# A three-pass graph kernel: destinations compared once per block, and groups taken in pairs in the third pass

## The chip, the cores and the metric

The kernel runs on one core of one Trainium2 chip. The metric is device time in microseconds from start to end on that core. The engines are named as the profile names them: PE is TensorE (matmul; its weight loads are PEld), DVE is VectorE, ACT is ScalarE, POOL is GpSimd, and SP is SyncE, which here only issues DMAs. Each engine works through its own queue in order. They wait for one another through semaphores, counters that an instruction raises when it is done.

## The reference

Two graph layers run over 30000 nodes of 128 features and 960000 edges, all in float32. The edges are sorted by destination.

```
h  = relu(layernorm(x))
# layer 0: a relation convolution with 32 edge types, used twice
W   = einsum('rb,bdf->rdf', coeff, basis)            # 32 matrices out of 8
agg = segment_sum((h @ W[etype])[src] * weight, dst) + bias
h1  = relu(agg(h; basis1, coeff1));   x = x + agg(h1; basis2, coeff2)
# layer 1: a gate with 4 edge types t
h   = relu(layernorm(x))
eta = sigmoid((h @ Wk[t] + bk[t])[dst] + (h @ Wq[t] + bq[t])[src])
out = x + mean over t of (segment_sum(eta * (h @ Wv[t] + bv[t])[src], dst) + h @ Ws[t] + b[t])
```

## The kernel before

Each of the two relation convolutions and the gate is one pass over all edges. A tile is 128 edges, a group is 3 tiles (G = 3, 384 edges), and a block is 5 groups (S = 5). One iteration of a pass's hardware loop holds 20 blocks (100 groups), cut into 4 stages of 25 groups; there are 25 iterations. Because edges are sorted, the destinations of a group lie in a window of 32 neighbouring nodes (W = 32) that starts at a number read from memory, its base.

**A relation pass** (`rel_body`, lines 415 to 541). For each group POOL gathers the source rows of 3 tiles with an indirect DMA each (line 511, recorded at line 118 in the helper), into `hg`, which has five buffers. DVE makes for each tile a matrix `sb` of 128 edges by 8 x 32 columns (line 515): where an edge's destination `relc` equals the column number `iw`, it holds the edge's coefficient `ce`, else 0. PE multiplies `hg` with `sb` and sums the 3 tiles in PSUM, in `pa` (line 520). ACT copies `pa` into `ab` (line 524). After the second group of a block PE runs `bases_out` for the block before (line 479): 8 matmuls with the basis matrices into `po`. At the fourth group DVE adds `po` of two blocks ago onto the node array `agg`, five windows (`add_windows`, line 413). The `sb` pool has 12 buffers, four groups.

In the first pass the edge types of a block are also loaded (`types`, line 436, four DMAs with 512-byte rows), compared with the type numbers (`onehot`, line 444) and multiplied with the coefficients (line 449) at the fourth group. That matmul writes the columns `pc` of a PSUM tile `cp`; the column numbers `iw` lie in the same tile, as do the partition numbers `ic`. The coefficients of the second pass are stored along the way and loaded back there (`keep`, `kept`).

**The gate pass** (`gate_body`, lines 543 to 631). For each group SP loads 128 rows of keys (`window`, line 560), five groups ahead. PE picks the key of each edge with a one-hot matrix (`keys`, line 577) into `pk`, which has four buffers. POOL gathers query and value (`qv`, ten buffers, line 614, again recorded at line 118). DVE adds the query (line 618), ACT takes the sigmoid (line 619). Two groups later DVE multiplies with the value (`msg`, line 586) and PE sums by destination into `po` (line 588). The order in DVE's queue is thus: add of group n, msg of group n-2; once a block also a one-hot comparison of 1920 columns with the destination matrix `sel` of 480 columns (lines 564, 570), and the five window adds.

All three passes run node steps beside the edges (`beside`): every 9 groups a unit of 120 nodes is turned, normalised, multiplied or stored, a few instructions per group. The order of the instructions on each engine is the order in which the program writes them; the framework adds only the semaphores. [...] The relation passes use `po` 2, `pa` 3, node steps 2 and `cp` 1; the gate pass uses `pk` 4, `po` 2, node steps 1 and `cp` 1.

Of the kernel before, what the change touches and what calls it, by code (L numbers as in the profile page):

```python
# [9 lines left out]
F32 = mybir.dt.float32  # L10
# [3 lines left out]
ALU = mybir.AluOpType  # L14
# [35 lines left out]
NX = N + LAG  # L50
LEAD = 3 * VB
GAP = 8
EPS = 1e-5
CH = 5
PX, KX = 120, 10
# [17 lines left out]
def kernel(  # L73
# [261 lines left out]
    def sorted_path():  # L335
# [5 lines left out]
        with ExitStack() as all_:  # L341
            def edge_pass(name, body, after, banks, extra=None):


                with ExitStack() as held:
                    weights = held.enter_context(tc.tile_pool(name=f"{name}_w", bufs=1))
                    steps, run = after(weights), body(weights)
                    with tc.tile_pool(name=f"{name}_io", bufs=NQ) as io, \
                            tc.tile_pool(name=f"{name}", bufs=2) as pool, \
                            tc.tile_pool(name=f"{name}_n", bufs=1) as npool, \  # L350
                            tc.tile_pool(name=f"{name}_nps", bufs=banks, space=PSUM) as nps, \
                            tc.tile_pool(name=f"{name}_c", bufs=1, space=PSUM) as cps, \
                            tc.tile_pool(name=f"{name}_ps", bufs=2, space=PSUM) as ps:
                        cp = cps.tile([P, 4 * D], F32, name="cp")
                        iw, ic = cp[:, :W], cp[:, W:W + 1]
                        nc.vector.tensor_copy(iw, irow)
                        nc.vector.tensor_copy(ic, icol)
                        with tc.For_i(0, NI, 1, iteration_sync="staggered") as i:
                            with tc.manual_schedule():
                                todo = {}  # L360
                                for n, step_ in extra(i, npool) if extra else ():
                                    todo.setdefault(n, []).append(step_)
                                for u in range(NPI // VB):
                                    at = i * -NPI + (N + LAG - (u + 1) * VB)
                                    for n, step in steps(at, npool, nps, 2):
                                        todo.setdefault(u * PERIOD + n, []).append(step)
                                assert W < TQ * 8 * B and max(todo) < NG

                                def beside(n):
                                    for step in todo.get(n, ()):  # L370
                                        step()

                                run(i, io, pool, ps, cp, iw, ic, beside)
                    left = LAG // VB
                    with tc.tile_pool(name=f"{name}_l", bufs=left) as lpool, \
                            tc.tile_pool(name=f"{name}_lps", bufs=8, space=PSUM) as lps:
                        for together in zip(*(steps(at, lpool, lps, left)
                                              for at in range(0, LAG, VB))):
                            for _, step in together:
                                step()  # L380
# [34 lines left out]
            def rel_body(table, weights, second):  # L415
                def start(npool):
                    bas = npool.tile([P, B, D], F32, name="bas")
                    nc.scalar.dma_start(bas, weights.rearrange("b d f -> d b f"))
                    return lambda *args: body(bas, *args)

                def body(bas, i, io, pool, ps, cp, iw, ic, beside):
                    stage = {}
                    er, oh, pc, ce, ce_next, ab, po, base = {}, {}, {}, {}, {}, {}, {}, {}

# [7 lines left out]

                    def types(s):
                        er[s] = pool.tile([P, TQ, TP], I32, name="er")
                        for c in range(TQ):
                            nc.sync.dma_start(
                                er[s][:, c, :],
                                bass.AP(tensor=et32_row.tensor,
                                        offset=(i * NG + s * S) * GE + c * TP,
                                        ap=[[TQ * TP, 4], [0, R], [1, TP]]))  # L440

                    def onehot(s):
                        oh[s] = pool.tile([P, TQ, TP], F32, name="oh")
# [30 lines left out]
                        nc.sync.dma_start(ce[s].rearrange("p t b -> p (t b)"), block_rows(s))  # L474

                    def bases_out(s):
                        po[s] = ps.tile([P, S, W], F32, name="po")
                        for b in range(B):
                            nc.tensor.matmul(po[s].rearrange("p s w -> p (s w)"),  # L479
                                             lhsT=bas[:, b, :],  # L480
# [13 lines left out]
                    for s in range(NS):  # L494
# [9 lines left out]
                        if s + 2 < NS:  # L504
                            (kept if second else types)(s + 2)
                        ab[s] = pool.tile([P, B, S, W], F32, name="ab")
                        for g in range(S):
                            t0 = (s % SB * S + g) * G
                            hg = pool.tile([TP, G, D], F32, name="hg", bufs=5)
                            for j in range(G):  # L510
                                gather(hg[:, j, :], table, idx[:, t0 + j:t0 + j + 1])
                            pa = ps.tile([P, B, W], F32, name="pa", bufs=3)
                            for j in range(G):
                                sb = pool.tile([TP, B, W], F32, name="sb", bufs=12)
                                nc.vector.scalar_tensor_tensor(  # L515
                                    sb, iw[:TP].unsqueeze(1).to_broadcast([TP, B, W]),
                                    relc[:, t0 + j:t0 + j + 1],
                                    ce[s][:, g * G + j, :].unsqueeze(2).to_broadcast([TP, B, W]),
                                    op0=ALU.is_equal, op1=ALU.mult)
                                nc.tensor.matmul(pa.rearrange("p b w -> p (b w)"),  # L520
                                                 lhsT=hg[:, j, :],
                                                 rhs=sb.rearrange("p b w -> p (b w)"),
                                                 start=(j == 0), stop=(j == G - 1))
                            nc.scalar.copy(ab[s][:, :, g, :], pa)  # L524
                            if g == 1 and s:
# [17 lines left out]
            def gate_body(i, io, pool, ps, cp, iw, ic, beside):  # L543
# [28 lines left out]
                        relc.unsqueeze(2).to_broadcast([TP, S * G, W]), ALU.is_equal)  # L572

                def keys(n):
                    pk[n] = ps.tile([TP, G, D], F32, name="pk", bufs=4)
                    for j in range(G):
                        nc.tensor.matmul(pk[n][:, j, :],  # L577
                                         lhsT=oh[n // S][:, n % S, j * TP:(j + 1) * TP],
                                         rhs=kw[n], start=True, stop=True)

                def sums(n):
                    s, g = n // S, n % S
                    if g == 0:
                        po[s] = ps.tile([P, S, W], F32, name="po")
                    msg = pool.tile([TP, G, D], F32, name="msg", bufs=3)
                    nc.vector.tensor_mul(msg, pk[n], qv[n][:, :, 1, :])  # L586
                    for j in range(G):
                        nc.tensor.matmul(po[s][:, g, :], lhsT=msg[:, j, :],  # L588
                                         rhs=sel[s][:, g * G + j, :],
                                         start=(j == 0), stop=(j == G - 1))  # L590

                loads(0)
                types(0)
                for n in range(S):
                    window(n)
                onehot(0)
                keys(0)
                for n in range(NG):
                    s, g, k = n // S, n % S, n // NGS
                    if n % NGS == 0:  # L600
                        if n:
                            tc.stage_boundary()
                        if k + 1 < NQ:
                            loads(k + 1)
                    if g == 0 and s % SB == 2:
                        leave_stage()
                    if g == 0 and s + 1 < NS:
                        types(s + 1)
                    if n + S < NG:
                        window(n + S)  # L610
                    qv[n] = pool.tile([TP, G, 2, D], F32, name="qv", bufs=10)
                    t0 = n % NGS * G
                    for j in range(G):
                        gather(qv[n][:, j].rearrange("p a f -> p (a f)"), qvtab,
                               stage[k][1][:, t0 + j:t0 + j + 1])
                    if n + 1 < NG:
                        keys(n + 1)
                    nc.vector.tensor_add(pk[n], pk[n], qv[n][:, :, 0, :])  # L618
                    nc.scalar.activation(pk[n], pk[n], AF.Sigmoid)  # L619
                    if n > 1:  # L620
                        sums(n - 2)
                    if g == 1 and s + 1 < NS:
                        onehot(s + 1)
                    if g == 4 and s:
# [1 line left out]
                    if g == 4 and s % SB == 0:  # L626
                        base[k] = bases(stage[k][0], DVE)
                    beside(n)
                sums(NG - 2)
                sums(NG - 1)  # L630
                add_windows(po[NS - 1], base[NQ - 1], NS - 1)


# [171 lines left out]

            edge_pass("c1", rel_body(h0, basis[0], False), after_first, 2, codes)
            edge_pass("c2", rel_body(h1, basis[1], True), after_second, 2)
            edge_pass("g", lambda weights: gate_body, after_third, 1)


    def any_path():
# [229 lines left out]
```

## Time and profile before

| what | value |
|---|---|
| time, median of 3 runs | 33966.85 us (33952.1 to 33968.91) |
| profiled execution, its own time | 34363.18 us |
| span in that profile | 34361.4 us |
| mean granted TensorE clock | 0.675; about 0.74 and 0.78 in the first two passes, 0.51 in the third |
| first pass, first to last gather | 169.6 to 11547.9 us |
| second pass | 11580.4 to 22583.7 us |
| third pass | 22630.1 to 34330.1 us |
| DMA | 0.24 to 0.25 of the 16 engines in the relation passes, 0.41 in the gate pass |
| gathers | 15000 rows-of-512-byte and 7500 rows-of-1024-byte gathers, 0.946 and 0.945 us each on POOL |

The table of groups has the engine's busy time, the mean duration in ns of one instruction, and the idle time of the engine just before such instructions with what ended most of it. Successive records of one engine can overlap a little, so the distance from start to start can be shorter than the duration. "remote" marks a wait whose end the trace puts down to no record that stands close to it. Durations of PE are modelled, and a PE record says when the array was given the work; when other engines learn of its end is seen only from their own starts and from the semaphore updates.

### The profile page before, as it was taken

To read this page: it belongs to the slowest core of one execution; us is meant where nothing else is said; L and a number is where in the kernel's file an instruction comes from. 1 tells how busy PE (TensorE), PEld (TensorE's weight loads), DVE (VectorE), ACT (ScalarE), POOL (GpSimd) and SP (SyncE) were. 2 spreads that over 40 slices of the span, in tenths; PEclk is the share of its full clock that TensorE was granted. 3 is DMA by queue.
4 is the path that set the end of the run, shared out by engine and by line. 5 is a ranking of instruction groups with operands and counts; after the bars stand their busy time and mean duration, and the time that the engine had idled before them with its cause. 6 is when DMAs were issued, how large, how long until landed. Compare 5 with 4: busy or idle time off the path is not lost.

```text
span 34361.4 us, 321543 instructions
## 1 busy us (share of the span) xinstructions
PE 19886.4 (58%) x83304; PEld 16933.4 (49%) x83304; DVE 12399.5 (36%) x32695; ACT 3636.0 (11%) x9834; POOL 21304.2 (62%) x22514
## 2 busy tenths in 40 slices
PE   4555555555555566656656666555555555555555
PEld 3444444444444444444444444445555555555555
DVE  4333333333333333333333333333333333333333
ACT  1000000000000011111111111111111111111111
POOL 5666666666666666666666666656656666666665
PEclk7777777777777777777777777765555555555555
DMA  3222222222222222222222222234444444444443
GB/s 100 64 63 63 64 64 64 63 64 63 63 63 63 66 65 66 65 66 65 66 65 66 65 66 65 65 105 123 122 121 121 121 121 122 122 123 121 121 122 118
DMA packets 2171202, 2914.97 MB, mean 85 GB/s; under 512 B 684764, under 2 KB 1617880, under 8 KB 2169544
## 3 DMA queue, kind: packets, MB, share of 16 engines
q0 software_dynamic: 840000, 1967.52, 21.0%
q1 hardware_dynamic: 923347, 651.19, 6.5%
q10 hardware_dynamic: 406197, 276.11, 2.8%
q8 instruction: 802, 13.14, 0.2%
q14 instruction: 856, 7.01, 0.1%
HBM read 2618.79 MB, written 274.16 MB: 84 GB/s over the span
## 4 chain that ended last, share of the span: by engine, by line


## 5 line engine op out<-in xcount | busy, mean ns | idle before, releaser
L118 POOL DMA_INDIRECT hg<-h,idx x15000 | 14189.1, 946 | 8366.8 <-issue 4281.9
L520 PE MATMUL pa<-sb,hg 128*128 128x256 f32 x30000 | 9211.6, 464 | 6063.6 <-issue 3309.4
L520 PEld LDWEIGHTS pa<-sb,hg 128*128 128x128 f32 x30000 | 6897.0, 239 | 7881.0 <-issue 3785.8
L118 POOL DMA_INDIRECT qv<-qvtab,qi x7500 | 7088.1, 945 | 4658.3 <-issue 2317.6
L515 DVE SCALAR_TENSOR_TENSOR sb<-cp,relc,ce 128x256 f32<-128x256 f32 x15000 | 6132.8, 475 | 5165.4 <-remote 3864.0
L588 PE MATMUL po<-sel,msg 128*128 128x32 f32 x15000 | 3459.4, 387 | 4659.8 <-DVE msg L586 3274.0
L588 PEld LDWEIGHTS po<-sel,msg 128*128 128x128 f32 x15000 | 3417.7, 327 | 4956.1 <-DVE msg L586 3424.9
L577 PE MATMUL pk<-kw,oh 128*128 128x128 f32 x15000 | 3965.9, 438 | 332.2 <-DVE oh L564 284.4
L618 DVE TENSOR_TENSOR pk<-pk,qv 128x384 f32<-128x384 f32 x2500 | 1407.4, 563 | 7030.1 <-remote 5356.4
L524 ACT COPY ab<-pa 128x256 f32<-128x256 f32 x5000 | 1809.0, 373 | 20007.9 <-remote 10336.1
L577 PEld LDWEIGHTS pk<-kw,oh 128*128 128x128 f32 x15000 | 3460.6, 330 | 334.9 <-issue 334.9
L479 PE MATMUL po<-ab,bas 128*128 128x160 f32 x16000 | 2456.1, 308 | 275.1 <-ACT ab L524 144.6
L479 PEld LDWEIGHTS po<-ab,bas 128*128 128x128 f32 x16000 | 2381.7, 198 | 384.4 <-ACT ab L524 169.6
L413 DVE TENSOR_TENSOR agg<-agg,po 128x32 f32 x7500 | 1401.6, 187 | 2827.7 <-remote 699.9
L619 ACT ACTIVATE pk<-pk 128x384 f32<-128x384 f32 x2500 | 1185.8, 475 | 9327.1 <-DVE pk L618 5397.8
L715 PE MATMUL bank<-wall,hT 128*120 128x512 f32 x1524 | 1052.1, 814 | 1083.9 <-ACT hT L711 338.1
L586 DVE TENSOR_TENSOR msg<-pk,qv 128x384 f32<-128x384 f32 x2500 | 1368.1, 547 | 126.8 <-remote 94.6
L449 PE MATMUL cp<-coeff,oh 128*128 128x64 f32 x4000 | 693.9, 306 | 964.1 <-issue 769.6
L449 PEld LDWEIGHTS cp<-coeff,oh 128*128 128x128 f32 x4000 | 687.4, 233 | 1019.3 <-issue 902.4
L564 DVE TENSOR_TENSOR oh<-kb,cp 128x1920 f32<-128x1920 bf16 x500 | 1072.2, 2144 | 47.5 <-issue 31.9
L715 PEld LDWEIGHTS bank<-wall,hT 128*120 128x120 f32 x1524 | 346.5, 246 | 1429.1 <-issue 627.9
L726 DVE TENSOR_TENSOR kt<-bank,ball 120x512 f32<-120x512 f32 x254 | 175.7, 692 | 2336.7 <-PE bank L715 895.3
(77 smaller groups left out, 3396.7 us busy)
## 6 DMA issues: line engine op xcount, KB each, us to landing
hg<-h,idx POOLq DMA_INDIRECT x15000
kb<-kcode SPq DMA_DIRECT2D x500, 480.0 KB
kw<-ktab SPq DMA_DIRECT2D x2500, 64.0 KB
er<-in_et_row SPq DMA_DIRECT2D x2000, 64.0 KB
qvtab<-qvt ACTq DMA_DIRECT2D x254, 480.0 KB
qv<-qvtab,qi POOLq DMA_INDIRECT x7500
ktab<-kt ACTq DMA_DIRECT2D x254, 240.0 KB
ce<-ce ACTq DMA_DIRECT2D x500, 60.0 KB
```

Of the source, the lines that this page charges most:

```text
L118: nc.gpsimd.indirect_dma_start(out=to, out_offset=None, in_=table, in_offset=bass.IndirectOffsetOnAxis(ap=idx, axis=0))
L413: nc.vector.tensor_add(to, to, po[:, g, :])
L449: nc.tensor.matmul(pc[s][:, c].rearrange("p q l b -> p (q l b)"), lhsT=oh[s][:, c, :], rhs=coeff.rearrange("p q l b -> p (q l b)"), start= ...
L479: nc.tensor.matmul(po[s].rearrange("p s w -> p (s w)"), lhsT=bas[:, b, :], rhs=ab[s][:, b].rearrange("p s w -> p (s w)"), start=(b == 0), ...
L515: nc.vector.scalar_tensor_tensor(sb, iw[:TP].unsqueeze(1).to_broadcast([TP, B, W]), relc[:, t0 + j:t0 + j + 1], ce[s][:, g * G + j, :].uns ...
L520: nc.tensor.matmul(pa.rearrange("p b w -> p (b w)"), lhsT=hg[:, j, :], rhs=sb.rearrange("p b w -> p (b w)"), start=(j == 0), stop=(j == G ...
L524: nc.scalar.copy(ab[s][:, :, g, :], pa)
L577: nc.tensor.matmul(pk[n][:, j, :], lhsT=oh[n // S][:, n % S, j * TP:(j + 1) * TP], rhs=kw[n], start=True, stop=True)
L586: nc.vector.tensor_mul(msg, pk[n], qv[n][:, :, 1, :])
L588: nc.tensor.matmul(po[s][:, g, :], lhsT=msg[:, j, :], rhs=sel[s][:, g * G + j, :], start=(j == 0), stop=(j == G - 1))
L618: nc.vector.tensor_add(pk[n], pk[n], qv[n][:, :, 0, :])
L715: nc.tensor.matmul(bank(a, VB, T * D), lhsT=hT, rhs=wall[:, a].rearrange("p t f -> p (t f)"), start=True, stop=True)
```

## The change

In the relation passes the comparison of destination with column number is done once per block for all 15 tiles (`hits`, 480 columns, in a PSUM bank of its own), and one multiplication per group makes `sb` for 3 tiles at once. The `sb` pool has 4 buffers of 3 tiles instead of 12 of one. To free a bank, the two `po` tiles become two halves of one bank, `pb`. The types of a block are loaded with one DMA of 2048-byte rows instead of four of 512-byte rows.

In the gate pass `qv`, `pk` and `msg` hold two groups. `qv` has 5 of these buffers, `pk` 2 (two banks each), `msg` 2. Once per pair, at the odd group, the program runs in this order: msg and sums of the pair before, the keys of the two groups to come, the add and the sigmoid of this pair. Keys are loaded 7 groups ahead instead of 5 (`AHEAD`). Stages begin at even groups (`begins`), 0, 26, 50 and 76.

```diff
                 def body(bas, pos, hits, i, io, pool, ps, cp, iw, ic, beside):
...
                     def types(s):
                         er[s] = pool.tile([P, TQ, TP], I32, name="er")
-                        for c in range(TQ):
-                            nc.sync.dma_start(
-                                er[s][:, c, :],
-                                bass.AP(tensor=et32_row.tensor,
-                                        offset=(i * NG + s * S) * GE + c * TP,
-                                        ap=[[TQ * TP, 4], [0, R], [1, TP]]))
+                        nc.sync.dma_start(
+                            er[s].rearrange("p c e -> p (c e)"),
+                            bass.AP(tensor=et32_row.tensor, offset=(i * NG + s * S) * GE,
+                                    ap=[[TQ * TP, 4], [0, R], [1, TQ * TP]]))
...
                     def bases_out(s):
-                        po[s] = ps.tile([P, S, W], F32, name="po")
+                        po[s] = pos[s % 2]
...
+                        nc.vector.tensor_tensor(
+                            hits, iw[:TP].unsqueeze(1).to_broadcast([TP, S * G, W]),
+                            relc[:, t0:t0 + S * G].unsqueeze(2).to_broadcast([TP, S * G, W]),
+                            ALU.is_equal)
                         for g in range(S):
...
+                            sb = pool.tile([TP, G, B, W], F32, name="sb", bufs=4)
+                            of = slice(g * G, (g + 1) * G)
+                            nc.vector.tensor_mul(
+                                sb, hits[:, of, :].unsqueeze(2).to_broadcast([TP, G, B, W]),
+                                ce[s][:, of, :].unsqueeze(3).to_broadcast([TP, G, B, W]))
                             for j in range(G):
-                                sb = pool.tile([TP, B, W], F32, name="sb", bufs=12)
-                                nc.vector.scalar_tensor_tensor(
-                                    sb, iw[:TP].unsqueeze(1).to_broadcast([TP, B, W]),
-                                    relc[:, t0 + j:t0 + j + 1],
-                                    ce[s][:, g * G + j, :].unsqueeze(2).to_broadcast([TP, B, W]),
-                                    op0=ALU.is_equal, op1=ALU.mult)
                                 nc.tensor.matmul(pa.rearrange("p b w -> p (b w)"),
...
                 def keys(n):
-                    pk[n] = ps.tile([TP, G, D], F32, name="pk", bufs=4)
+                    if n % 2 == 0:
+                        pk[n // 2] = ps.tile([TP, 2, 4, D], F32, name="pk")[:, :, :G, :]
...
-                def sums(n):
...
+                def sums(m):
+
+                    msg = pool.tile([TP, 2, G, D], F32, name="msg")
+                    nc.vector.tensor_mul(msg, pk[m], qv[m][:, :, :, 1, :])
+                    for n in (2 * m, 2 * m + 1):
...
-                    if n + 1 < NG:
-                        keys(n + 1)
-                    nc.vector.tensor_add(pk[n], pk[n], qv[n][:, :, 0, :])
-                    nc.scalar.activation(pk[n], pk[n], AF.Sigmoid)
-                    if n > 1:
-                        sums(n - 2)
+                    if n % 2:
+                        if m:
+                            sums(m - 1)
+                        if n + 2 < NG:
+                            keys(n + 1)
+                            keys(n + 2)
+                        nc.vector.tensor_add(pk[m], pk[m], qv[m][:, :, :, 0, :])
+                        nc.scalar.activation(pk[m], pk[m], AF.Sigmoid)
```

## The prediction

> **What bounds the kernel now.** I read the page's engine shares first, then the groups by line, the time order inside a block, and last the waits of each pass. No engine is full: POOL has the largest share, 62%. Its groups say more:
>
> ```profile
> PE 19886.4 (58%) x83304; PEld 16933.4 (49%) x83304; DVE 12399.5 (36%) x32695; ACT 3636.0 (11%) x9834; POOL 21304.2 (62%) x22514
> L118 POOL DMA_INDIRECT hg<-h,idx x15000 | 14189.1, 946 | 8366.8 <-issue 4281.9
> L118 POOL DMA_INDIRECT qv<-qvtab,qi x7500 | 7088.1, 945 | 4658.3 <-issue 2317.6
> L515 DVE SCALAR_TENSOR_TENSOR sb<-cp,relc,ce 128x256 f32<-128x256 f32 x15000 | 6132.8, 475 | 5165.4 <-remote 3864.0
> L618 DVE TENSOR_TENSOR pk<-pk,qv 128x384 f32<-128x384 f32 x2500 | 1407.4, 563 | 7030.1 <-remote 5356.4
> L564 DVE TENSOR_TENSOR oh<-kb,cp 128x1920 f32<-128x1920 bf16 x500 | 1072.2, 2144 | 47.5 <-issue 31.9
> ```
>
> A gather takes 0.945 us and the next follows 0.305 us later at best, so 22500 gathers need 22500 x 1.249 = 28.1 ms of the 34.36 ms span. In the order of time the rest is stops of 2 to 5 us, about one for each block of 15 gathers. From first to last gather the passes take 11378, 11003 and 11700 us; above the pace of 1.249 us POOL stops for 1979, 1643 and 2328 us in them. In mid-iteration that is 3.5, 3.2 and 4.1 us a block; the first and third pass add some 8 and 13 us where an iteration begins. A change gains or loses time here only by changing these stops.
>
> What ends a stop shows in the time order of the first pass (start, duration, engine):
>
> ```profile
> 5003.41 2.75 PE L520 MATMUL pa<-sb,hg 128*128 128x256 f32 x12
> 5006.00 1.00 PE L449 MATMUL cp<-coeff,oh 128*128 128x64 f32 x8
> 5012.15 0.94 POOL L118 DMA_INDIRECT hg<-h,idx  x1 [0.30 <-issue]
> 5016.42 0.65 ACT L524 COPY ab<-pa 128x256 f32<-128x256 f32 x2 [14.61 <-remote]
> 5016.66 0.94 POOL L118 DMA_INDIRECT hg<-h,idx  x1 [3.56 <-remote]
> 5016.72 4.79 DVE L515 SCALAR_TENSOR_TENSOR sb<-cp,relc,ce 128x256 f32<-128x256 f32 x12 [14.68 <-remote]
> ```
>
> PE's twelve matmuls end at 5006.2, yet ACT, DVE and POOL, which wait for them, all go on only at 5016.4 to 5016.7. The trace's semaphore updates say why: 13 increments of PE's counter land 40 ns apart between 5016.19 and 5016.70. They came late together, 3.1 us after POOL's last gather had ended. This holds over the trace. In the first 4 us after POOL resumes a pa matmul is mostly seen by ACT 0.04 us after its end; from 6 to 8 us on it is seen late; about 3 us after POOL stops all late increments arrive at once. I call the late stretch "frozen". So a stop is about 3 us until the increments arrive, plus the work of other engines until POOL's buffer is free.
>
> **The skill.** "PSUM — Partial Sum Buffer", section Terms, says that TensorE's write and VectorE's access must not meet in one bank; programs therefore order them by bank. Above, DVE's sb for the fifth group (which reads iw from bank cp) starts 0.02 us after the last increment, that of the coefficient matmul into other columns of cp. The trace agrees, and I use the rule for the new shared banks. "VectorE: DVE Perf Modes", section Mode 1x (REGULAR), gives one result a cycle at 0.96 GHz, 1.04 ns, for fp32 tensor_tensor. Rows of one kind, sel (480 elements, 650 ns) and oh (1920, 2144 ns), give 1.04 ns an element plus 152 ns; I use these.
>
> **The change, part by part.**
>
> 1. *hits and sb.* Fifteen sb instructions a block, 0.392 us from start to start (4.79 us hold twelve), are 5.9 us. After: hits, 480 elements, 0.65 us; five products of 768 elements, 152 + 768 x 1.04 = 0.95 us, 0.87 from start to start: 5.0 us. That saves some 0.9 ms of DVE over 1000 blocks, beside 5165 us of idle time before sb: 0 on the path. Price without that cover: PE's first matmul of a group waits for 0.95 instead of 0.48 us of DVE, +0.5 us. sb keeps four groups of space.
>
> 2. *Who waits for a bank.* In the first pass sb of the fifth group no longer waits for the coefficient matmul of the fourth (the wait of 14.68 us above; remote waits before sb are 3178 us in this pass); hits of the next block does, one group later. New: both po lie in bank pb, so add_windows at the fourth group waits for bases_out that PE runs after the second. Behind it in DVE's queue is sb of the fifth group, then PE. The block gains a group of freedom and loses up to two. At a flood of increments DVE then does five adds (1.1 us) and a product (0.95) before PE's fifth group, where it did one sb (0.4): +1.6 us. POOL has two just freed groups, 7.5 us, to hide it. No row shows this wait: bound -0.3 to +0.4 us a block in the first pass and 0 to +0.2 in the second, where node steps already tie DVE to PE. I take 0 for both.
>
> 3. *One er load for four.* Three SP issues of 0.55 us a block go, with their register work; the bytes stay. In the frozen stretch SP's own instructions take 0.7 us each, so they may share what delays PE. The second pass, with one block load on SP, stops 0.3 us a block less, so the bound is 0 to -0.3 us: I take -0.1 x 500 = -50, and -50 where an iteration begins (six fewer issues, 3.3 us at most, x 25).
>
> 4. *Pairs in the third pass.* Add and msg over 768 elements: 0.95 us each for 2 x 0.563 and 2 x 0.547. Sigmoid: ACT copies of 256 and 512 elements take 373 and 594 ns, hence 0.82 us for 768 instead of 2 x 0.475. Busy time falls by 0.3 us (DVE) and 0.1 us (ACT) a pair, beside idle time: 0. PE's matmuls and counter increments are as many as before. What matters is the chain that frees qv. Before:
>
> ```profile
> 27205.95 0.57 DVE L618 TENSOR_TENSOR pk<-pk,qv 128x384 f32<-128x384 f32 x1 [5.32 <-remote]
> 27206.42 0.55 DVE L586 TENSOR_TENSOR msg<-pk,qv 128x384 f32<-128x384 f32 x1
> 27207.24 0.94 POOL L118 DMA_INDIRECT qv<-qvtab,qi  x1 [3.89 <-DVE msg L586]
> ```
>
> PE's increments arrive, DVE adds group n, then multiplies group n-2, whose sigmoid is long done, and POOL goes on 1.3 us after the arrival. After: gather of pair m+5 waits for msg(m), and DVE is held at add(m), so the chain is add 0.95, sigmoid 0.82 plus passing, msg 0.95, 0.25 to POOL: 3.0 us. One-hot and sel (2.8 us) or the adds (1.1 us) stand between add and msg in four of five pairs, 1.7 us on average instead of 0.85: 3.9 us. A stop grows from 4.1 to about 2.9 + 3.9 = 6.8 us. Against it, POOL is ten groups past the held add instead of eight, and PE may have one more pair of keys done when the increments arrive. Before, one stop serves five groups (4.1/5 = 0.82 us a group). After: two pairs at the arrival and one in the next 5 us, so six groups, 6.8/6 = 1.13; if a fourth pair gets through the frozen stretch, 6.8/8 = 0.85. Bound: +0.03 to +0.31 us a group, +75 to +775 us in 2500 groups. I take +300, nearer the low half since extra work overlaps waits. Where an iteration begins, msg(0) stands behind two groups of keys, a longer add and the second one-hot, together 2.6 us later: x 25 = +65.
>
> 5. *AHEAD 7, even stage starts.* Two more kw loads ahead on SP, none more in sum, ten buffers still; two more at an iteration's start lie behind the first loads and beside 13 us of waiting: 0. If kw were late it would be one landing per iteration, under 50 us.
>
> Sum: -50 - 50 + 300 + 65 = +265 us. Against the profiled execution's own 34363.2 us (span 34361.4 and 1.8 around it) that is 34628. The runs' median, 33966.9, is 396 us (1.2%) lower; the stops must be in those runs too, since gathers alone need 28.1 ms. I add the difference unchanged: 34230.
>
> **The rivals.**
>
> - *The third pass breaks even.* Four pairs a stop, +75 +65 - 100 is about +40: 34000. For it: the larger lead of POOL. Against: the longer chain.
> - *Faster.* Fewer semaphore updates ease what delays PE. Counted by the block (16 per gather by its 4-byte packets, about as many per wide load, one per engine instruction) the passes have about 360, 345 and 397, and stop for 1979, 1643 and 2328 us: some 13 us per update. The change takes 21, 9 and 8 away: about -500 us in all; with the longer chain of part 4 half left, -370: 33600. It decides if stops a block fall below 3.2 us in the first two passes. Against: three points and no mechanism shown.
> - *Much slower.* Bank pb's wait catches PE in the frozen stretch of most blocks, so POOL stops after four groups instead of five (3.5/4 - 3.5/5 = 0.18 us x 5000 = +875) and the third pass adds 265: 35100. It decides when the fifth group's matmuls come over 7.5 us after the flood.
> - *The change doesn't do what it says*: DVE's instructions fall by 9000 (sb) and 2500 (third pass) whatever happens to the time, so I give this no chance.
>
> **How the numbers follow.** Slower by the pair chain 0.50, with its own range 34060 to 34740 (part 4's ends); even 0.13; faster 0.26; much slower 0.11. A difference of 0.2%, 68 us, is about what these runs can tell. Hence faster 0.26, same 0.13, slower 0.61. The range 33550 to 34900 takes in the faster case and leaves out the far end of the much slower one.
>
> **What would show it.** The first two passes: DVE's busy time about 0.45 ms lower each, stops still one per block, 3.2 to 3.6 us; DVE's remote waits before the products much shorter, some now at the adds. The third: stops of 6 to 7 us after 18 or 24 gathers, ended by msg; gathers still 0.945 us. I am wrong if stops in the third pass stay near 4 us (the chain is hidden), if POOL runs past 15 gathers in the first two (an easier counter), or if TensorE's clock, 0.51 there, rises with runs of twelve matmuls.

## The result and the profile after

The changed kernel takes 34581.69 us (median of 4 runs, 34567.24 to 34606.2). Kernel before takes 33967.88 us beside it (median of 4, 33952.1 to 33980.53). The ratio is 1.0182, with an interval of 1.0168 to 1.0197: 614 us slower, where 34230 us, 263 us slower, was forecast. The sign is right and the time lies in the range, but the size is less than half of the loss.

Kernel before takes 28.4 to 28.5 ms on six of the seven chips that the experiments ran on, as does the changed kernel on the one of them where it ran whole, and the two take 34.0 and 34.6 ms again on the seventh, so times are compared only with those of kernel before on the same chip. On which chip this first measurement was made is not on record.

The page of the changed kernel has the lines that answer to those of before:

```profile
PE 19029.1 (55%) x83304; PEld 15977.8 (46%) x83304; DVE 11358.8 (33%) x21195; ACT 3455.8 (10%) x8584; POOL 21295.2 (62%) x22514
L119 POOL DMA_INDIRECT hg<-h,idx x15000 | 14173.3, 945 | 8085.4 <-issue 4257.4
L119 POOL DMA_INDIRECT qv<-qvtab,qi x7500 | 7094.9, 946 | 5146.4 <-issue 2270.4
L528 DVE TENSOR_TENSOR sb<-hits,ce 128x768 f32<-128x768 f32 x5000 | 4597.8, 949 | 562.3 <-issue 221.7
L641 DVE TENSOR_TENSOR pk<-pk,qv 128x768 f32<-128x768 f32 x1250 | 1203.6, 963 | 7560.4 <-remote 5907.1
L415 DVE TENSOR_TENSOR agg<-agg,pb 128x32 f32 x5000 | 939.9, 188 | 8029.6 <-remote 5368.8
L642 ACT ACTIVATE pk<-pk 128x768 f32<-128x768 f32 x1250 | 993.8, 795 | 10006.5 <-DVE pk L641 8820.9
```

VectorE has lost 1.04 ms of work and a third of its instructions, and the kernel as a whole is slower: the gathers still take 0.945 us each, and POOL's idle time before `hg` fell by 281 us while that before `qv` rose by 488 us. The new wait for the shared bank `pb` is there too, 5369 us at the adds; it took the place of the 3864 us before `sb`. (The counts beside `po`, `pa`, `pk` and `cp` in the description of the kernel are PSUM banks; in each pass they come to eight with those of the node steps.)

By pass, from first to last gather, the two profiles divide like this ("stops" is POOL's idle time above the pace of 1.249 us a gather):

| pass | before, us (stops) | after, us (stops) | difference |
|---|---|---|---|
| first relation pass | 11378 (1979) | 11114 (1737) | -264 |
| second relation pass | 11003 (1643) | 10970 (1605) | -33 |
| gate pass | 11700 (2328) | 12200 (2820) | +500 |

In the gate pass the stops fall from 730 to 422 in number, and those of more than 1 us grow from a mean of 3.48 to 6.68 us; 398 of 421 distances between stops are 18 gathers, six groups. Before, the commonest distance there was 12 gathers (365 of 657), four groups. One stop of the changed kernel in order of time (start, duration, engine):

```profile
28030.98 0.95 POOL L119 DMA_INDIRECT qv<-qvtab,qi  x1 [0.30 <-issue]
28035.20 0.97 DVE L641 TENSOR_TENSOR pk<-pk,qv 128x768 f32<-128x768 f32 x1 [17.34 <-remote]
28036.08 2.14 DVE L576 TENSOR_TENSOR oh<-kb,cp 128x1920 f32<-128x1920 bf16 x1
28036.21 0.80 ACT L642 ACTIVATE pk<-pk 128x768 f32<-128x768 f32 x1 [19.40 <-DVE pk L641]
28038.14 0.65 DVE L582 TENSOR_TENSOR sel<-cp,relc 128x480 f32<-128x480 f32 x1
28038.71 0.95 DVE L597 TENSOR_TENSOR msg<-pk,qv 128x768 f32<-128x768 f32 x1
28039.92 0.95 POOL L119 DMA_INDIRECT qv<-qvtab,qi  x1 [8.00 <-DVE msg L597]
```

POOL's last gather ends at 28031.9. The add, due long before, starts 3.3 us later, when TensorE's increments arrive: the trace has 15 of them 0.04 us apart, from 28035.10 to 28035.69 us. From there to POOL it is 4.7 us: add, the one-hot comparison and `sel` with the sigmoid beside them, msg. Before, the same way took 1.3 us.

Where is the rest of the 614 us? The profiled runs differ by 34567.2 - 34363.2 = 204 us only. The changed kernel's profiled run belongs to its timed runs (it is the fastest of the four). That of before was 395 us longer than its own. So either the gains of the relation passes in the table are partly an excess of that one execution, or the loss in the gate pass is larger than it shows. Apart from some 16 us (the changed kernel's median is 14 us above its profiled run), the 614 us divide so: if the 395 us lay wholly in the relation passes, the change costs +98 there and +500 in the gate pass; if wholly in the gate pass, -297 and +895. Anywhere between these two ends, the gate pass holds at least 500 us of the loss. No run settled the split (see the last experiments). One figure leans to the second end: the granted clock averages 0.675 in the profiled execution of before, and 0.678 to 0.680 in three timed runs of it on the later chip where it takes 34 ms. The gate pass has 0.51 and the other two 0.74 and 0.78, so, by an estimate from these figures, 395 us less in the gate pass would make 0.677 of it, and 395 us less in the relation passes 0.674. Runs of one kernel on one chip differ by 0.002 to 0.007 in this figure, so it is a hint and no more.

### The profile page after: what moved, and what is told of

It reads as the page before. It is cut to its first block, busy times and chain, and to the rows that moved or that the text cites. A ratio compares the mean times of both kernels' runs of the same rounds, so it can differ in the third digit from the quotient of the medians.

```text
span 34565.5 us, 290215 instructions
## 1 busy us (share of the span) xinstructions
PE 19029.1 (55%) x83304; PEld 15977.8 (46%) x83304; DVE 11358.8 (33%) x21195; ACT 3455.8 (10%) x8584; POOL 21295.2 (62%) x22514
## 4 chain that ended last, share of the span: by engine, by line
## 5 line engine op out<-in xcount | busy, mean ns | idle before, releaser
L603 PE MATMUL po<-sel,msg 128*128 128x32 f32 x15000 | 2810.2, 352 | 4312.8 <-DVE msg L597 4192.2
L603 PEld LDWEIGHTS po<-sel,msg 128*128 128x128 f32 x15000 | 2783.8, 283 | 4609.2 <-DVE msg L597 4471.0
L528 DVE TENSOR_TENSOR sb<-hits,ce 128x768 f32<-128x768 f32 x5000 | 4597.8, 949 | 562.3 <-issue 221.7
L641 DVE TENSOR_TENSOR pk<-pk,qv 128x768 f32<-128x768 f32 x1250 | 1203.6, 963 | 7560.4 <-remote 5907.1
L415 DVE TENSOR_TENSOR agg<-agg,pb 128x32 f32 x5000 | 939.9, 188 | 8029.6 <-remote 5368.8
L487 PE MATMUL pb<-ab,bas 128*128 128x160 f32 x16000 | 2411.8, 305 | 130.8 <-ACT ab L536 73.6
L487 PEld LDWEIGHTS pb<-ab,bas 128*128 128x128 f32 x16000 | 2351.1, 195 | 228.7 <-ACT ab L536 100.8
L642 ACT ACTIVATE pk<-pk 128x768 f32<-128x768 f32 x1250 | 993.8, 795 | 10006.5 <-DVE pk L641 8820.9
L597 DVE TENSOR_TENSOR msg<-pk,qv 128x768 f32<-128x768 f32 x1250 | 1189.1, 951 | 396.9 <-ACT pk L642 232.4
L516 DVE TENSOR_TENSOR hits<-cp,relc 128x480 f32<-128x480 f32 x1000 | 663.9, 664 | 1204.2 <-remote 754.7
```

What stands on the lines that cost most here:

```text
L487: nc.tensor.matmul(po[s].rearrange("p s w -> p (s w)"), lhsT=bas[:, b, :], rhs=ab[s][:, b].rearrange("p s w -> p (s w)"), start=(b == 0), ...
L528: nc.vector.tensor_mul(sb, hits[:, of, :].unsqueeze(2).to_broadcast([TP, G, B, W]), ce[s][:, of, :].unsqueeze(3).to_broadcast([TP, G, B, W]))
L597: nc.vector.tensor_mul(msg, pk[m], qv[m][:, :, :, 1, :])
L603: nc.tensor.matmul(po[s][:, g, :], lhsT=msg[:, n % 2, j, :], rhs=sel[s][:, g * G + j, :], start=(j == 0), stop=(j == G - 1))
L641: nc.vector.tensor_add(pk[m], pk[m], qv[m][:, :, :, 0, :])
```

## The experiments

**The parts alone.** Each is kernel before with one part of the change:

```diff
  # relation passes only                         # third pass only
+ hits once a block, sb per group, pb, one er    - qv, pk, msg per group, S windows ahead
  gate_body as before                            + qv, pk, msg per pair, AHEAD = 7
  # one er load only: types() with one dma_start instead of four
  # deeper: the changed kernel with qv bufs=7 pairs instead of 5
```

> Only the relation passes are changed (one comparison per block, the product per group, both po in one bank, one er load); the gate pass is that of before. Theory: the two traces show the first pass 264 us and the second 33 us shorter, and that holds in timed runs: 33968 - 300 = 33670, all in the first pass, where stops at the fourth group go. Rival 1: the relation part is worth nothing in timed runs, and the whole +614 is the pairs': 33970 within 70. Rival 2: bank pb's wait costs in timed runs what the profile does not show: above 34040.

> Only the gate pass is changed (pairs, keys 7 groups ahead, even stage starts). Theory: the pairs lose what the relation part gains and the 614 besides: 33968 + 900 = 34870, with stops of 6 to 7 us after 18 gathers in the third pass. Rival: they cost what the two profiles show between third passes, 12200 - 11700 = 500: 34470. A third pass of before that is as long here as in its first profile (11700) speaks for the rival, one near 11300 for the theory.

> Only the four type loads of a block become one, in the first pass. Theory: SP's instructions share what delays TensorE's increments, so nine fewer a block shorten stops by 0.1 to 0.3 us and the start of an iteration by 2: -50 to -200 us, 33770 to 33920. Rival: the gain of the first pass comes from the comparison alone: 33968 within 50.

> The changed kernel with seven qv pairs instead of five, nothing else. Theory: a stop keeps its 6.7 us (arrival of the increments, then add, sigmoid, msg), but POOL may run 14 groups past the held add instead of 10, so a stop comes after 24 gathers or more instead of 18: 6.7/8 instead of 6.7/6 us a group, -700 us: 33880. Rival: how far the increments let DVE get, not the buffers, sets the run of POOL: stops stay at 18 gathers on average and the time within 70 of 34582.

Measured beside 28478.96 us for before: relation passes 28502.77 us, ratio 1.0009 (1.0000 to 1.0017); third pass 28475.06 us, 0.9999 (0.9990 to 1.0008); one load 28492.88 us, 1.0005 (0.9996 to 1.0014); deeper 28632.63 us, 1.0054 (1.0037 to 1.0071). None of the theories had a case for this: POOL hardly stops. In the three parts alone its stops come to 0 to 60 us a pass; 22500 x 1.249 us is all there is. The deeper `qv` costs instead of gaining: its trace has one stop of 5.3 us at the first gather of every iteration of the third pass but the first, 24 x 5.3 = 127 us of the 154 us lost. The other 24 or so are what the relation passes alone lost on this chip.

**The whole again, and before again.**

> The changed kernel itself, once more, beside the kernel before on one chip. In the four runs before this one POOL never stops and the kernel before takes 28479 us instead of 33968: the late increments, on which the whole forecast rests, were not there. Theory: the pairs and the relation part only change how long a stop lasts, so without stops this run is within 70 us of before (28.45 to 28.55 ms); with the late increments, at some 34 ms, it is 500 to 700 us above before. Rival: the two parts cost something together that neither costs alone: over 100 us above before without stops.

> The kernel before with a profile on the same chip as the run beside it, so that the two traces can be compared. Theory: SP's register instructions take 0.04 to 0.07 us at all times where POOL doesn't stop, and 0.7 us in stretches where it does; TensorE's increments are late in the second case only. Rival: increments are as late as in the first profile, and something else (POOL's buffers) hides it here.

28470.66 us beside 28443.53, ratio 1.0009 (1.0000 to 1.0018); before, profiled, 28440.54 us. So what differs between 34 and 28.4 ms is not the kernel. POOL's waits of the two executions of the changed kernel show it. First the 34.6 ms one, then this one (total us, times, longest):

```profile
POOL hg L119 <- remote: 2290.4, 825, 4.5
POOL qv L119 <- DVE msg L597: 2231.9, 330, 16.0
POOL hg L119 <- PE pa L532: 1127.3, 660, 16.5
```

```profile
POOL hg L119 <- PE pa L532: 370.2, 1138, 3.0
POOL hg L119 <- DMA hg<-h,idx: 240.6, 672, 3.0
POOL qv L119 <- DMA qi<-qidx: 39.9, 1, 39.9
```

The 330 waits for msg, 2232 us in sum, are gone from POOL's large waits, and so is "remote". The chain itself is still there, as long as forecast, in the gate pass of the faster execution:

```profile
24027.21 0.97 DVE L641 TENSOR_TENSOR pk<-pk,qv 128x768 f32<-128x768 f32 x1 [4.59 <-DMA qv<-qvtab,qi]
24028.21 0.80 ACT L642 ACTIVATE pk<-pk 128x768 f32<-128x768 f32 x1 [6.58 <-DVE pk L641]
24029.07 0.95 DVE L597 TENSOR_TENSOR msg<-pk,qv 128x768 f32<-128x768 f32 x1
```

Add to the end of msg is 2.8 us, but the add starts when the gather has landed, not late, and POOL has other pairs to gather meanwhile. The instruments agree: the traces of the faster executions hold 560382 and 541503 semaphore updates (before, after), those of the first measurement 147921 and 170743, of the same two kernels.

**The parts a second time, and what lies behind the gathers.** Two thin kernels leave out two gathers of three, so that POOL no longer bounds:

```diff
                             for j in range(G):
-                                gather(hg[:, j, :], table, idx[:, t0 + j:t0 + j + 1])
+                                if j == 0:
+                                    gather(hg[:, j, :], table, idx[:, t0 + j:t0 + j + 1])
...
-                                                 lhsT=hg[:, j, :],
+                                                 lhsT=hg[:, 0, :],
  # the gate pass alike: one gather a group, its tile taken for all three
```

> The changed relation passes (one comparison a block, products of whole groups, adds from one bank, one load of er) with the third pass of before, on another chip. Theory: the change has a price only where the increments of the semaphores come late, as in the first profiles (before 34.0 ms). If this chip shows before near 34.0 ms, the relation part alone gains about 0.3 ms (the two traces: 264 + 33 us less waiting of the gathers), 33650 to 33750 us, and the pairs have to cost more than the whole. If it shows before near 28.45 ms the ratio is 0.999 to 1.001. Rival: the relation part also costs where increments are late, its adds waiting for the bank: 34000 to 34200 us beside 34.0 ms.

> The third pass of the changed kernel alone, on the same chip as the relation part alone. Theory: where before takes near 34.0 ms, pairs cost 0.5 ms and more, 34500 to 34950 us, with stops of 6 to 7 us after 18 gathers; where before takes near 28.45 ms the gathers never stop and the ratio is 0.999 to 1.001. Rival: pairs are as dear as groups by group and the loss of the whole came from the passes together; then 34.0 ms +- 0.1.

> Kernel before with one gather of three left out of it, or rather two of three: each group gathers its first tile only, and the products and sums use that tile three times (the output is not the reference's). It takes the bound of the gathers away: 7500 of them, 9.4 ms of GpSimd. What is then left is the next bound: TensorE with 21.4 ms busy in the trace of before (DVE 12.4 ms). Expected 21 to 24 ms, the third pass at least 7.1 ms.

> The changed kernel with the same two of three gathers left out (the output is not the reference's). Theory: behind the gathers the change is worth little either way, TensorE being next: within 1% of the thin kernel before in the relation passes (VectorE's 1.0 ms less is beside TensorE), and in the third pass faster by up to 0.9 ms (TensorE busy 7.1 to 6.2 ms there, in longer runs). Rival, that of the forecast: the longer chain of add, sigmoid and product of pairs costs as soon as nothing hides it: the third pass 0.3 to 0.9 ms longer than in the thin kernel before.

Relation passes 28443.58 us beside 28419.19, 1.0008 (1.0001 to 1.0015); third pass 28418.36, 1.0000 (0.9991 to 1.0009): as in the first batch. The small loss is in the first pass: two stops in each iteration, 0.9 to 1.3 us at the 16th gather and 1.0 us around the 56th, where the kernels with the old relation passes stop 0.3 and 0.2 us. The one load of `er` alone shows the second of them and not the first.

Thin before takes 18177.99 us, thin after 17372.75 (two runs each): 805 us, 4.4%, faster. Both are below the 21 ms expected: TensorE's clock in the relation passes is 0.97, where it was 0.84 to 0.86 with all gathers, and its busy time falls from 21.4 to 16.7 ms. The clock is part of that: it would take the 14.3 ms of the relation passes to an estimated 12.6, and 10.4 were measured. By pass, from first to last gather: 5517, 5834 and 6530 us before, 5618, 6192 and 5240 after. So behind the gathers the relation passes lose 101 and 358 us (2 and 6%, where less than 1% was expected), and the pairs, which were to be the dear part, gain 1290. VectorE's saved work brings no gain in the relation passes, where TensorE is busy 89 to 92% of the time. The gain of the third pass goes with TensorE's clock. Groups of thin before and thin after, each with the clock in 40 slices of the span:

```profile
PEclk9999999999999999999999999755555555555555
L578 PE MATMUL pk<-kw,oh 128*128 128x128 f32 x15000 | 3914.4, 433 | 139.5 <-DVE oh L565 139.5
L589 PE MATMUL po<-sel,msg 128*128 128x32 f32 x15000 | 3269.7, 374 | 113.1 <-DVE msg L587 113.1
```

```profile
PEclk9999999999999999999999999999888888887878
L604 PE MATMUL po<-sel,msg 128*128 128x32 f32 x15000 | 2182.1, 301 | 772.1 <-DVE msg L598 770.7
L591 PE MATMUL pk<-kw,oh 128*128 128x128 f32 x15000 | 2452.9, 326 | 136.1 <-DVE oh L577 136.1
```

The same matmuls, as many of them, take 433 and 374 ns before and 326 and 301 ns after. TensorE even waits longer for msg, 771 instead of 113 us: that is the longer chain, and it is small.

**What raises the clock, what lengthens the relation passes, and the whole a third time.** One thin kernel puts the new bank into the old relation passes; one puts the old turns of matmuls into the new third pass:

```diff
  # one bank: thin before
-                        po[s] = ps.tile([P, S, W], F32, name="po")
+                        po[s] = pos[s % 2]
  # alternate: thin after, in sums(m)
                     for n in (2 * m, 2 * m + 1):
+                        if n % 2 and 2 * m + 4 < NG:
+                            keys(2 * m + 4)
```

> The thin kernel before (two of three gathers left out, the output is not the reference's), with one edit: the sums of the bases of the relation passes go by turns into the two halves of one bank, as in the changed kernel, and not into two banks. Measured so far: thin before 18178 us, its relation passes 5517 and 5834 us from first to last gather; thin after 5618 and 6192 us, with 1067 us of adds waiting for the bank's matmuls. Theory: the shared bank is what makes the relation passes of the thin changed kernel 0.1 and 0.36 ms longer; then this one has 5600 and 6150 us there, 18.5 to 18.65 ms in all, the third pass at 6530 us. Rival: the wide product (three tiles in one instruction, so that the first matmul of a group waits for all three) makes them longer; then this one is at 18180 us +- 60.

> The thin changed kernel (two of three gathers left out, the output is not the reference's), with one edit in its third pass: the matmuls are issued in the old turns, three sums, three keys, three sums, three keys, while the add, the sigmoid and the product stay on pairs. Measured so far: third pass 6530 us in thin before at a clock of 0.55, 5240 us in thin after at 0.85, keys 433 to 326 ns. Theory: the clock, and with it the gain, comes from the matmuls standing six and six; then this third pass is near 6.4 ms at 0.5 to 0.6 and the whole at 18.4 to 18.7 ms. Rival: it comes from the wide VectorE and ScalarE instructions and the pauses that they leave TensorE; then the third pass stays at 5.2 to 5.4 ms at 0.8 or more and the whole at 17.3 to 17.5 ms.

> The changed kernel again on another chip. Theory: where the increments come in time (before near 28.45 ms) 28470 us +- 60, ratio 0.999 to 1.003; where they come late (before near 34.0 ms) 34500 to 34700 us, ratio 1.015 to 1.022. Rival: the loss belongs to the change and not to the late increments; then 1.01 or more on any chip.

This was the chip on which before takes 34 ms (33968.49 us, 33936.68 to 33973.77), and the changed kernel took 34629.28 us, ratio 1.0197 (1.0168 to 1.0227). The loss recurs, with gate pass stops of 6.74 us after 18 gathers in 396 of 423 cases and passes of 11118, 10988 and 12230 us. The rival, that the loss is the change's on any chip, is out.

The alternate order took 18733.72 us. Its relation passes, 5623 and 6190 us, are those of thin after within 0.1%; its third pass is 6635 us, against 5240, at the clock of before:

```profile
PEclk9999999999999999999999999855555555555555
L591 PE MATMUL pk<-kw,oh 128*128 128x128 f32 x15000 | 4021.1, 442 | 135.2 <-DVE oh L577 135.2
L606 PE MATMUL po<-sel,msg 128*128 128x32 f32 x15000 | 3320.2, 378 | 90.4 <-DVE msg L598 90.4
```

So the order of the matmuls decides: six sums and six keys in turn, or three and three (each is two records in the trace). The wide VectorE instructions, which both kernels have, do not. That these relation passes agree between two chips of which one takes 34 ms with all gathers says something else as well: with POOL busy 38% of the time, nothing comes late enough on that chip to cost time. (Its trace still lacks semaphore updates: 220495 here, 301378 in thin after.)

One bank took 18256.02 us, relation passes 5541 and 5908 us, that is +24 and +74 us of the +101 and +358. The shared bank is about a fifth of it, so this theory falls for the larger part. That the product of three tiles holds TensorE's first matmul is only argued: in the second pass TensorE waits 125 us for `sb` in thin after (110 times) and 23 us in thin before (once). In that pass the `pa` matmuls are also longer, 398 ns each instead of 389, 165 us in sum. Why, and the rest, is open.

**The split where POOL stops.** These runs take a part alone, or before under a profile, to other chips, to meet that condition again.

> The third pass of the changed kernel with the relation passes of before, on another chip. Measured where before takes 33968 us: the changed kernel 34582 and 34629 us, its third pass 12200 and 12230 us. Theory: there the relation part gains some 300 us as the two profiles say (11378 to 11114 and 11003 to 10970 us) and the pairs lose some 900: 34800 to 34950 us, relation passes of 11380 and 11000 us in its trace. Rival: the profiled execution of before was 395 us longer than its timed runs in these same passes, so that the relation part is worth nothing: 34500 to 34650 us, with relation passes of about 11100 and 10950 us. Where before takes near 28.45 ms: 0.999 to 1.001.

> The same kernel as in the run before (the third pass of the changed kernel, the relation passes of before), on another chip. Where before takes near 34.0 ms: theory 34800 to 34950 us with relation passes of 11380 and 11000 us in its trace; rival 34500 to 34650 us with relation passes of about 11100 and 10950 us. Where before takes near 28.45 ms: ratio 0.999 to 1.001.

> Kernel before once more with a profile. In the first measurement its profiled execution took 34363 us, its timed runs 33967 us. Open is in which pass the 395 us lie. Where this chip shows before near 34.0 ms: theory, they lie in all passes alike and a profile of 33970 us has about 11250, 10880 and 11570 us from first to last gather; rival, they lie in the relation passes, 11100 and 10900 us, and the third keeps 11700 us. Where it shows 28.45 ms: passes of 9360 to 9430 us, no stops.

> The changed relation passes with the third pass of before, on another chip. Where before takes near 34.0 ms: theory 33650 to 33750 us (relation passes of 11114 and 10970 us as in the profile of the changed kernel, third pass of 11700 us as in the profile of before, less what that profile was too long); rival, the relation part is worth nothing against timed runs: 33920 to 34050 us, with a third pass near 11600 us. Where before takes near 28.45 ms: ratio 1.000 to 1.002.

> The third pass of the changed kernel with the relation passes of before, on another chip. Where before takes near 34.0 ms: theory 34800 to 34950 us with relation passes of 11380 and 11000 us in its trace; rival 34500 to 34650 us with relation passes of about 11100 and 10950 us. Where before takes near 28.45 ms: ratio 0.999 to 1.001.

All fell on chips where POOL does not stop. The third pass alone: 0.9999 (0.9989 to 1.0008), 1.0000 (0.9990 to 1.0010) and 1.0000 (0.9990 to 1.0010). The relation passes alone: 1.0009 (0.9999 to 1.0019). Before once more: 28466.65 us beside 28464.76. So the split of the 614 us stays between the two ends given above. On these chips the gathers' own pace is the time, and no part of the change touches it.

## Why the prediction was right and wrong

**Durations: right.** Product 949 ns (forecast 950), add and msg 963 and 951 (950), sigmoid 795 (820), hits 664 (650). VectorE's busy time falls by 425 us in each relation pass (forecast 450).

**Parts 1 and 2, saved work and bank waits at 0, part 3, one load at -100: open.** The profiles say -297 us together, but up to 395 us can belong to before's profiled execution; on two chips without stops the three parts together cost 24 us. The bank's wait sits where it was expected, at the adds. "Much slower" is refuted: in the relation passes the commonest distance between stops is 15 gathers (350 and 366 times), not 12 (71 and 52 times). The reading "about one for each block of 15 gathers" did not hold for before: it has 1.3 to 1.4 stops of more than 1 us a block, and in its first pass distances of 9, 12 and 15 gathers are about as frequent (198, 195 and 183 times).

**Part 4, the pairs: mechanism right, size wrong.** Stops of 6.8 us after six groups were forecast, 6.68 us after six groups came, ended by msg. The price of this very case stood in the text: 6.8/6 = 1.13 us a group. The first step that failed is "I take +300, nearer the low half since extra work overlaps waits". In the last 17 blocks of an iteration the stops grow from 70.8 to 92.2 us, that is from 0.83 to 1.08 us a group, x 25 = +535 us where +300 was for the whole of it. The cost is 0.25 us a group: 0.12 was taken, and 0.31 was the upper end. The iteration's start, costed at +65, gives 45 us back: the first three blocks stop 20.9 us instead of 22.7, since the stops of the third block shrink from 17 to 7.4 us. Sum +490 in these blocks, +500 with the rest, against +365. The picture of before was off too, though not its price a group: its stops in this pass are 3.5 us long and mostly four groups apart, not 4.1 us and five groups.

**"I add the difference unchanged": wrong, and the larger miss.** Against the profiled execution the sum was +265 and +204 came. That is near in part by luck: the relation passes missed by -197 and the gate pass by +135, and these misses cancel. Against the timed runs the change cost +614. The 396 us between profile and timed runs were no constant of both kernels but an excess of that one execution, larger than the whole forecast effect: in the changed kernel the difference is 14 us, and of the other sign. The forecast fell short by 351 us: the two misses take off 62, and this step adds some 410. Which pass holds the excess was unknown when the forecast was made, and still is, so part of the 410 may be a further cost of the pairs; the difference should have stood in the range on one side only. The range given for the pair chain, 34060 to 34740, does not follow from part 4's ends either: with the terms of the sum they give 34007 to 34707.

**Rivals.** "Fewer semaphore updates", 13 us each, predicted -500 us. Its sign in the relation passes came: in the last 17 blocks of an iteration they stop 3.0 us a block, under the 3.2 that was to decide for it, where before stops 3.6 and 3.2. So -264 and -33 may be partly its work; this is not settled. But the timed runs leave it at most those 297 us, and the gate pass, with fewer updates too, went the other way. "Break-even" needed four pairs a stop; the trace has three (18 gathers) or two, never four.

**The clock.** "If TensorE's clock, 0.51 there, rises with runs of twelve matmuls" was named as a sign of error. It did rise, 0.51 to 0.59 in the gate pass (0.62 on a chip without stops). The pass before and after (stretch, its length, busy time of PE, PEld, DVE, ACT and POOL, clock, DMA share, GB/s):

```profile
22630.00:34330.00 11700.00, 6722.08 (x30164) 6423.57 (x30165) 4209.86 (x8471) 1327.80 (x3019) 7087.99 (x7500) 0.51 0.41 122
```

```profile
22328.00:34528.00 12200.00, 5991.74 (x30153) 5586.77 (x30153) 4015.03 (x5973) 1134.68 (x1770) 7094.88 (x7500) 0.59 0.40 117
```

It isn't what made the time wrong: TensorE waits for gathers in both kernels. It is the change's only gain of size, and the gathers hide it.

## What to carry to other kernels

When several buffers are served by one stop, price a longer chain by stop length over groups served, and discount that value only for an overlap that a trace shows: here 0.31 us a group was computed, 0.12 taken and 0.25 measured. Before a sum made on a profiled execution is carried to timed runs, see whether the two agree; a gap of 1.2% is an unknown of that size. Work saved behind a bound engine shows no gain until the bound is lifted, as on the chips where POOL does not stop; a kernel with part of the bound left out shows at once what then counts, which here was TensorE's clock, a thing that the forecast only named.

## What was not expected of the hardware

- **Increments that come late on one chip of seven.** By chip, the kernel before takes 28.42 to 28.48 ms or 33.97 ms, both steady within 0.3%. Where it is 34 ms, TensorE's increments arrive in floods after POOL has stopped (15 within 0.6 us in the stop shown above), and the trace holds a quarter to a third of the semaphore updates. SyncE's register instructions take 0.71 us at the 90th percentile in the first profile of before, and 0.07 us at the 99th where before takes 28.4 ms. The gathers take 0.945 us in both. With two gathers of three left out that chip takes as long as another: thin after's relation passes agree within 0.1%, and the third pass of one bank, the same as in thin before, takes 6488 us there and 6530 us on the other. What causes it no run shows.
- **A busy TensorE at half its clock.** The third passes of thin before, thin after and alternate (columns as above):

```profile
11602.00:18133.00 6531.00, 6291.74 (x30143) 6259.23 (x30144) 4233.47 (x8466) 1329.45 (x3017) 2367.87 (x2500) 0.52 0.40 117
```

```profile
12058.00:17298.00 5240.00, 4345.91 (x30152) 4211.27 (x30153) 4001.80 (x5975) 1134.78 (x1771) 2361.64 (x2500) 0.82 0.51 146
```

```profile
12060.00:18695.00 6635.00, 6421.17 (x30134) 6410.07 (x30135) 4050.25 (x5974) 1134.19 (x1770) 2364.44 (x2500) 0.51 0.40 116
```

TensorE is busy 96 and 97% of the time at 0.52 and 0.51, and 83% at 0.82. In each of the three passes its records leave only 25 gaps of more than 3.4 us, one an iteration. The Trainium skill, "TensorE: Matmul & The Clock Gate", Part 1, lets the clock rise to full after some 3.4 us of activity and fall after as much idleness. In this case the measurement decides: a larger share of busy time does not bring the higher clock, and the order of the matmuls moves it. (A slower clock also makes each matmul longer, so part of the busy share is its effect.) Why, no run shows.
- **More buffers that cost.** Seven pairs of `qv` instead of five bring a stop of 5.3 us at each iteration's start, and the kernel takes 0.5% more than before.
